# Moving output statistics, fusion and two projections within a hand-ordered schedule of attention and scans

## The chip, the cores and the metric

One core of a Trainium2 chip runs one program for the whole computation. The metric is the device time of one execution in microseconds (us), as the median of several runs. The engines are named as in the profile: PE (matmuls), DVE (vector), ACT (activations), POOL (GpSimd) and SP, whose queue issues the DMAs.

## The reference, cut to what matters

x is (8, 512, 48, 48), that is 8 samples of 512 channels by L = 2304 positions. Two layers follow each other, each with a group norm in front and a residual around it:

```python
# layer 0: linear causal attention, 8 heads of 64
Q = elu(Wq gn(x)) + 1;  K = elu(Wk gn(x)) + 1;  V = Wv gn(x)
S_t = S_{t-1} + k_t v_t^T;   o_t = (q_t S_t) / (q_t . cumsum(K)_t)
x = x + o
# layer 1: gn(x) in 4 blocks of 128 channels, one after the other
for i in range(4):
    x_i = spx[i] + prev                      # prev: the fused result of block i - 1
    xz = x_i @ Wi;  xp, z = split(xz)
    xs = silu(causal_conv4(xp));  dt, B, C = xs @ Wx
    delta = softplus(dt @ Wdt + b)
    h_t = exp(delta_t A) h_{t-1} + delta_t xs_t B_t      # 256 channels x 16 states
    y = (sum_n h_t C_t + xs D) * silu(z);  x_m = y @ Wo
    fg = max(x_i, x_m)
    prev = sigmoid(mean(x_i)) * x_i + sigmoid(mean(fg)) * fg
x = x + concat(prev of the four blocks)
```

The recurrence over positions is what DVE's scan instruction computes. The sigmoids' means are sums over all positions of a block, so a block's fusion starts only when all of its chunks are through; the next block of that sample starts from it. In the group norm in front of layer 1 each block needs the statistics of layer 0's output over all positions.

## The kernel before, in words

Positions are cut into NC = 6 chunks of LC = 384. The second layer's work comes in **jobs**: one chunk of one block of one sample, 8 x 4 x 6 = 192 jobs. A job has SLOTS = 8 **slots** (`slot(k)`), and a slot four scans of 128 x 384 (`scan`, L830). Each slot's body also makes, for slots ahead, the decays (`decay`, L819, an exponential on ACT into a PSUM bank), the products of B and delta x (`product` on DVE, L809, for most columns, `last_product` on POOL, L798, for the last 128), and behind the scans the weighing with C (`weigh`, L846, POOL), whose sum over states PE gathers into the one accumulator yp (`gather`, L853). yp is opened by the skip product (`skip`, L787, ACT) and emptied by the gate (`gated`, L865, DVE), twice a job. Two streams of samples take turns by job, so that one's fusion lies beside the other's scans.

Everything else is a *task*: a generator that yields where it may go on. A slot has two **halves**, and `beside(half)` is called in each, ahead of the first scan and behind the second; it lets each task that is due emit its next stage. `(t, gap), n` means: not before half t, at least gap halves after the last stage, with n free PSUM banks; a string of a digit is a gap alone. What is emitted this way stands in the engines' queues in that order, and no scheduler changes it. Half 0 to half 15 below are the halves of a job.

PSUM has six free banks, `take()`n and given back by tasks and decays. `ahead(DEPTH)` emits up to three decays ahead, as far as banks are there. Stores are kept in a list by `save` and issued on SP two halves later by `flush`.

The tasks that matter here:

- `chunk(m)` is layer 0 for one chunk of one block. `times[m]` is its first half, and falls into half 3 of a job in the steady part (a period of 16 halves); `at(j)` is half times[m] + j. It projects q, k and v (`project`, L286, three PSUM banks), forms q and k with an exponential and a relu on ACT (`feature`, L298 and L299) and a min and add on DVE (q L343, k L351), turns and sums (L362, L379), masks (L434) and adds the result to the input: `xr` at L450, its `bn_stats` at L452. After a block's last chunk `group_norm` aggregates them (L169), averages over 16 channels on PE (L171, L186), takes the power on POOL (L191) and leaves scale and shift (L195).
- `Stream.pass_on` fuses the finished block and prepares the next one's input xi, chunk by chunk: three DMA loads (xb, fu, xo; L569 to L574), scalings on ACT (L596, L597, L601), and additions on POOL (L604, L609, L612), or, for the first block of a sample, a normalization on ACT in place of L609 (L607). For a chunk c > 0 its times are given by `first`, the first half of the job that will need it.
- `Job.prepare` makes a later job's inputs: the conv (L635) and the gate's projection (L646) on PE, silu (L671 to L676, with a table load ahead of them and one behind) near half 14, the softplus (L706, again two table loads) near half 3, then the products of delta and xs on POOL (L747) and the loads of B, C, dr and dxr.
- `finale(job)` projects y with Wo (`project`, L871) and takes the maximum and its sum (`maximum`, L882). It is begun in half 4 of the next job, behind the last gate.

Of the kernel before, what the change touches and what calls it, by code (L numbers as in the profile page):

```python
# [49 lines left out]
def attention_then_mamba_kernel(  # L50
# [18 lines left out]
    B, _, L = x.shape  # L69
# [84 lines left out]
    def save(out, in_):  # L154
        stores.append((half_no[0], out, in_))

    def flush(every=True):
        while stores and (every or stores[0][0] <= half_no[0] - 2):
            _, o, i = stores.pop(0)
            nc.sync.dma_start(out=o, in_=i)  # L160
# [46 lines left out]
    norms, xns, x1s, done, ksums = {}, {}, {}, {}, {}  # L207
# [58 lines left out]
    def chunk(m):  # L266


        b, o, c = parts[m]
# [3 lines left out]
        cols, tile_rows = slice(c * LC, (c + 1) * LC), slice(o * P, (o + 1) * P)  # L273
# [3 lines left out]
        def at(j, gap=1):  # L277
            return times[m] + j, gap

        def new(tag, bufs=1, shape=(P, LC)):  # L280
            return apool.tile(list(shape), F32, tag=tag, name=f"{tag}_{n}", bufs=bufs)

        def project(j):
            ps = bank()[:, 0:LC]
            for kt in range(4):
                nc.tensor.matmul(  # L286
                    ps,
                    wq_sb[:, kt, j * 512 + o * P : j * 512 + (o + 1) * P],
                    xn[:, kt, :],
                    start=(kt == 0),  # L290
                    stop=(kt == 3),
                )
            return ps, bqkv_sb[:, j * 4 + o : j * 4 + o + 1]

        def feature(ps, bias):

            ex = new("ex", 2)
            nc.scalar.activation(ex, ps, AF.Exp, bias=bias)  # L298
            nc.scalar.activation(ps, ps, AF.Relu, bias=bias)  # L299
            return ex  # L300
# [31 lines left out]
        S, stats, ksum = passes[b, o]  # L332
# [5 lines left out]
        qp, qb = project(0)  # L338
        yield at(1), 0
        ex = feature(qp, qb)  # L340
        yield at(2), 0
        q = new("q", 2)
        nc.vector.scalar_tensor_tensor(q, ex, 1.0, qp, ALU.min, ALU.add)  # L343
        bank.free()
        yield at(2, 0), 1
        kp, kb = project(1)
        yield at(3), 0
        ex = feature(kp, kb)
        yield at(4), 0
# [73 lines left out]
        xr = new("xr")  # L423
# [25 lines left out]
        yield at(24), 0  # L449
        nc.vector.tensor_add(xr, xr, ops)  # L450
        bank.free()
        nc.vector.bn_stats(stats[:, 0, c, :], xr)  # L452
        save(x1s[b][tile_rows, cols], xr)
        if c + 1 == NC:
            norm = yield from group_norm(
                stats, 1, f"m{b}_{o}", 8, [(times[m] + j, 1) for j in (28, 29, 29, 30, 31)]
            )
            flush()
            done[b, o] = norm

    class Stream:
# [62 lines left out]
        def pass_on(self):  # L524


            xi = self.xi
            old = None
            if self.b is not None:
                old = self.b, self.s, self.n, self.fm  # L530
                wt = small.tile([P, 4], F32, tag="wt", name=f"wt_{self.n}")
                nc.vector.tensor_copy(wt[:, 2:3], self.sums)
                nc.vector.tensor_reduce(wt[:, 3:4], self.fsum, AX.X, ALU.add)
            last = old is not None and old[1] == 3 and not self.samples
            if not last:
                self.move_on()
                while (self.b, self.s) not in done:
                    yield "1w", 0
                norm = done[self.b, self.s]
            s = self.s  # L540
            if old is not None:
                yield "1", 0

                nc.scalar.activation(wt[:, 0:2], wt[:, 2:4], AF.Exp, scale=-1.0 / L)
                yield "1", 0
                nc.vector.tensor_scalar_add(wt[:, 0:2], wt[:, 0:2], 1.0)
                nc.vector.reciprocal(wt[:, 0:2], wt[:, 0:2])
            else:
                yield "1", 0
            if not last:  # L550
                if self.fresh:
                    self.sums = norm[:, 2, :]
                else:

                    sums = small.tile([P, 2], F32, tag="sums", name=f"sums_{self.n}", bufs=3)
                    nc.vector.tensor_scalar(
                        sums[:, 0:1], wt[:, 2:3], wt[:, 0:1], norm[:, 2, :], ALU.mult, ALU.add
                    )
                    nc.vector.tensor_scalar(
                        sums[:, 1:2], wt[:, 3:4], wt[:, 1:2], sums[:, 0:1], ALU.mult, ALU.add  # L560
                    )
                    self.sums = sums[:, 1:2]

            def loads(c):
                fu = xb = xa = None
                cols = slice(c * LC, (c + 1) * LC)
                if not last:
                    xb = mpool.tile([P, LC], F32, tag="xb", name=f"xb_{self.n}_{c}")
                    nc.sync.dma_start(out=xb, in_=x1s[self.b][s * P : (s + 1) * P, cols])  # L569
                if old is not None:  # L570
                    fu = mpool.tile([P, LC], F32, tag="fu", name=f"fu_{old[2]}_{c}")
                    nc.sync.dma_start(out=fu, in_=old[3][:, cols])
                    xa = mpool.tile([P, LC], F32, tag="xo", name=f"xo_{old[2]}_{c}")
                    nc.sync.dma_start(out=xa, in_=x1s[old[0]][old[1] * P : (old[1] + 1) * P, cols])  # L574
                return fu, xb, xa

            now = loads(0)
            for c in range(NC):

                if c and not last:  # L580
                    first = 2 * self.jobs[self.block * NC + c].start
                    yield (first - 36, 1), 0
                    now = loads(c)
                    yield (first - 30, 1), 0
                elif c:
                    yield "3", 0
                    now = loads(c)
                    yield "1", 0
                else:
                    yield "1", 0  # L590
                cols, icols = slice(c * LC, (c + 1) * LC), slice(3 + c * LC, 3 + (c + 1) * LC)
                fu, xb, xa = now
                if not last:
                    normed = dict(bias=norm[:, 1, :], scale=norm[:, 0, :])
                if old is not None:
                    nc.scalar.activation(fu, fu, AF.Copy, scale=wt[:, 1:2])  # L596
                    nc.scalar.activation(xi[:, icols], xi[:, icols], AF.Copy, scale=wt[:, 0:1])  # L597
                if old is None:
                    nc.scalar.activation(xi[:, icols], xb, AF.Identity, **normed)
                elif not last and not self.fresh:  # L600
                    nc.scalar.activation(xb, xb, AF.Identity, **normed)  # L601
                if old is not None:
                    yield "1", 0
                    nc.gpsimd.tensor_tensor(fu, fu, xi[:, icols], ALU.add)  # L604
                    yield "1", 0
                    if not last and self.fresh:
                        nc.scalar.activation(xi[:, icols], xb, AF.Identity, **normed)  # L607
                    elif not last:
                        nc.gpsimd.tensor_tensor(xi[:, icols], xb, fu, ALU.add)  # L609
                    self.ready = c + 1  # L610
                    yield "1", 0
                    nc.gpsimd.tensor_tensor(xa, xa, fu, ALU.add)  # L612
                    save(out[old[0], old[1] * P : (old[1] + 1) * P, cols], xa)
                self.ready = c + 1

    class Job:
# [250 lines left out]
        def project(self):  # L867
            self.bank = Banks()
            self.xm = self.bank()
            for h in range(2):  # L870
                nc.tensor.matmul(  # L871
                    self.xm[:, 0:LC],
                    self.w[2][:, h, :],
                    self.yz[:, h, :],
                    start=(h == 0),
                    stop=(h == 1),
                )
# [72 lines left out]
    parts, times = [], []  # L950
# [4 lines left out]
            parts.append((b, o, c))  # L955

    def finale(job):
        yield "0", 1
        job.project()
        yield "1", 0  # L960
        job.maximum()
        if job.c == NC - 1:
            yield from job.stream.pass_on()
# [4 lines left out]
    for b in counted:  # L968
        first = times[parts.index((b, 0, 0))]
# [59 lines left out]
    def at(k):  # L1029
        return jobs[k // SLOTS], k % SLOTS  # L1030
# [22 lines left out]
    def close(k):  # L1053

        job = at(k)[0]
        while waiting:
            waiting.pop(0)()
        job.gated(1)
        job.closed = True
        tasks.insert(0, Task(finale(job)))  # L1060
# [140 lines left out]
```

## Time and profile before

| | |
|---|---|
| median of 3 runs | 9154.76 us (9140.69 to 9157.51) |
| profiled execution, its own time | 9167.14 us |
| its span | 9165.3 us |
| granted TensorE clock, mean | 0.961 |
| DVE scans, L830 | 6144, 5471.0 us, 939 ns each |
| POOL weighing, L846 | 1536, 4880.6 us, 3177 ns each |
| ACT decays, L819 | 6144, 3432.3 us, 579 ns each |
| ACT table loads for L819, L671, L706 | 382, 192, 192, 1283 ns each |
| DVE statistics of the output, L452 | 192, 107.6 us, 560 ns each |
| HBM traffic | 178 GB/s over the span |

A group of instructions is given by its line, engine and operation. The table of waits says which engine waited, with the line of the instruction that waited and that of the one that released it, then the sum in us, the number of waits and the longest. In a timeline each row has a start and a duration in us, and idle time ahead of it in brackets.

### The profile page before, as it was taken

What the parts mean: (1) busy time and instruction counts of PE and PEld (TensorE: products, weight loads), DVE (VectorE), ACT (ScalarE), POOL (GpSimd) and SP (SyncE); (2) the same over time, 40 slices, a digit from 0 to 9 for tenths busy, and PEclk for the clock granted to TensorE, in tenths of its full rate; (3) what the DMA queues carried; (4) which work ended last, traced back from release to release, by engine and by line L of the source; (5) the groups of instructions that cost most, each with busy time, mean ns of one, the idle gap of its engine ahead of it and who ended that gap; (6) DMA issues with size and microseconds to landing.
All of it is one profiled execution on the core that took longest, in us unless ns stands there. A gap on an engine that the chain in (4) does not pass through costs nothing.

```text
span 9165.3 us, 120476 instructions
## 1 busy us (share of the span) xinstructions
PE 7631.5 (83%) x35714; PEld 3602.8 (39%) x35714; DVE 8342.1 (91%) x11640; ACT 6579.4 (72%) x12656; POOL 8066.8 (88%) x5635
## 2 busy tenths in 40 slices
PE   7888888888888888888888888888888888888865
PEld 4443444433344444443333444444333444444321
DVE  3899999999999999999999999999999999999997
ACT  2677777777777777777777777777777777777775
POOL 1788989899988899899998888998999898989998
PEclk9999999999999999999999999999999999999977
DMA  5566666666766666666666666666666666666654
GB/s 182 161 173 180 185 184 184 181 188 180 196 173 179 184 186 187 183 180 181 191 184 182 174 178 187 187 184 184 180 188 183 181 179 177 178 178 177 164 156 129
DMA packets 1002898, 1642.84 MB, mean 179 GB/s; under 512 B 138592, under 2 KB 797312, under 8 KB 1002240
## 3 DMA queue, kind: packets, MB, share of 16 engines
q1 hardware_dynamic: 1002240, 1635.13, 65.0%
q8 instruction: 283, 4.64, 0.2%
q14 instruction: 375, 3.07, 0.1%
HBM read 1309.06 MB, written 325.58 MB: 178 GB/s over the span
## 4 chain that ended last, share of the span: by engine, by line
DVE 31%; ACT 21%; PE 18%; POOL 10%; DMA 9%; issue 8%; SPq 3%; POOLq 0%; DVEq 0%; ACTq 0%
DVE u L830 20%; ACT bank L819 7%; PE bank L635 6%; POOL u L846 6%; DVE u L809 6%; PE bank L286 5%; ACT L819 4%; PE yp L853 3%; PE bank L646 3%; POOL u L798 2%; DMA C<-scr 2%; ACT L706 2%; ACT bank L299 1%; DMA B<-scr 1%; SPq L739 1%
## 5 line engine op out<-in xcount | busy, mean ns | idle before, releaser
L830 DVE TENSOR_TENSOR_SCAN u<-bank,u 128x385 f32<-128x385 f32 (+1 forms) x6144 | 5471.0, 939 | 378.3 <-ACT bank L819 331.9
L846 POOL TENSOR_TENSOR u<-u,C 128x1536 f32<-128x1536 f32 x1536 | 4880.6, 3177 | 216.4 <-DVE gm_m L175 83.2
L819 ACT ACTIVATE bank<-dr,av 128x385 f32<-128x385 f32 (+1 forms) x6144 | 3432.3, 579 | 1406.9 <-DVE u L830 1118.1
L853 PE MATMUL yp<-u,cst 128*64 128x384 f32 x12288 | 2429.2, 516 | 505.7 <-ACT yp L787 263.9
L798 POOL TENSOR_TENSOR u<-B,dxr 128x512 f32<-128x512 f32 x1536 | 1958.8, 1275 | 21.4 <-DMA dxr<-xscr 16.9
L809 DVE TENSOR_TENSOR u<-B,dxp 128x1024 f32<-128x1024 f32 x1536 | 1835.0, 1195 | 9.4 <-ACT dxp L782 9.4
L286 PE MATMUL bank<-xn,wq_sb 128*128 128x384 f32 x4608 | 1730.3, 520 | 97.1 <-DVE u L830 40.4
L853 PEld LDWEIGHTS yp<-u,cst 128*64 128x64 f32 x12288 | 781.0, 139 | 1713.3 <-issue 1051.6
L635 PE MATMUL bank<-xi,wk 128*128 128x384 f32 x3072 | 1122.1, 509 | 306.1 <-ACT kl L383 234.3
L286 PEld LDWEIGHTS bank<-xn,wq_sb 128*128 128x128 f32 x4608 | 870.0, 199 | 894.6 <-DVE u L830 153.6
L635 PEld LDWEIGHTS bank<-xi,wk 128*128 128x128 f32 x3072 | 563.0, 193 | 878.2 <-ACT kl L383 351.5
L844 POOL COPY state<-u 128x4 f32<-128x4 f32 x1280 | 241.7, 189 | 538.4 <-DVE u L830 522.7
L298 ACT ACTIVATE ex<-bank,bqkv_sb 128x384 f32<-128x384 f32 x384 | 219.6, 572 | 520.1 <-PE bank L286 491.6
L747 POOL TENSOR_TENSOR delta<-delta,xs 128x384 f32<-128x384 f32 x384 | 384.6, 1002 | 141.6 <-DMA dscr<-delta 124.6
L819 ACT ACT_TABLE_LOAD x382 | 490.1, 1283 | 6.7
L787 ACT ACTIVATE yp<-xs,pv 128x384 f32<-128x384 f32 x384 | 222.7, 580 | 373.2 <-DVE yz L865 373.2
L871 PE MATMUL bank<-yz,wo 128*128 128x384 f32 x768 | 307.0, 517 | 55.5 <-DVE yz L865 36.7
L695 PE MATMUL bank<-dbc,wd 9*128 9x384 f32 x768 | 302.2, 513 | 3.2 <-ACT dbc L687 3.2
L646 PE MATMUL bank<-xi,wi 128*128 128x384 f32 x768 | 289.2, 498 | 14.3 <-ACT xs L671 14.3
L416 PE MATMUL bank<-cst,rdb 128*128 128x128 f32 x576 | 103.2, 290 | 228.3 <-DVE u L830 226.1
L447 PE MATMUL bank<-sm,v 128*64 128x128 f32 x2304 | 260.9, 305 | 33.8 <-DVE u L830 30.6
L682 PE MATMUL bank<-xs,wx 128*40 128x384 f32 x768 | 281.3, 489 | 0.8 <-DVE sm L434 0.8
(109 smaller groups left out, 7632.7 us busy)
## 6 DMA issues: line engine op xcount, KB each, us to landing
B<-scr SPq DMA_DIRECT2D x1536, 192.0 KB
C<-scr SPq DMA_DIRECT2D x1536, 192.0 KB
xn<-xn SPq DMA_DIRECT2D x192, 768.0 KB
dr<-dscr SPq DMA_DIRECT2D x768, 192.0 KB
dxr<-xscr SPq DMA_DIRECT2D x768, 192.0 KB
dscr<-delta SPq DMA_DIRECT2D x192, 384.0 KB
xscr<-delta SPq DMA_DIRECT2D x192, 384.0 KB
xn<-in_x SPq DMA_DIRECT2D x48, 768.0 KB
```

The lines of the kernel that those rows point to most:

```text
L286: nc.tensor.matmul(ps, wq_sb[:, kt, j * 512 + o * P : j * 512 + (o + 1) * P], xn[:, kt, :], start=(kt == 0), stop=(kt == 3),)
L635: nc.tensor.matmul(xc, wk[:, k, h * P : (h + 1) * P], xi[:, c0 + k : c0 + k + LC], start=(k == 0), stop=(k == 3),)
L646: nc.tensor.matmul(zp, wi[:, 256 + h * P : 256 + (h + 1) * P], xi[:, c0 + 3 : c0 + 3 + LC], start=True, stop=True,)
L695: nc.tensor.matmul(vp, wd[32:41, h * P : (h + 1) * P], dbc[32:41, :], start=True, stop=True)
L747: nc.gpsimd.tensor_tensor(delta[:, h, :], delta[:, h, :], xs[:, h, :], ALU.mult)
L798: nc.gpsimd.tensor_tensor(u[:, :, :, 1 + LC - TAIL :], self.B[s % 4][:, :, cols].unsqueeze(2).to_broadcast(shape), self.dxr[s // 4][:, :, ...
L809: nc.vector.tensor_mul(u[:, :, :, 1 : 1 + LC - TAIL], self.B[s % 4][:, :, cols].unsqueeze(2).to_broadcast(shape), self.dxp.unsqueeze(1).to ...
L819: nc.scalar.activation(dA[:, cols], self.dr[h][:, g, cols], AF.Exp, scale=self.w[6][:, 2 * h + g, q + j : q + j + 1],)
L830: nc.vector.tensor_tensor_scan(u[:, j, g, cols], dA[:, cols], u[:, j, g, cols], 0.0, ALU.mult, ALU.add,)
L846: nc.gpsimd.tensor_tensor(h, h, self.C[s % 4].unsqueeze(2).to_broadcast([P, NG, 2, LC]), ALU.mult)
L853: nc.tensor.matmul(self.yp[g * 64 : g * 64 + 64, 0:LC], pair_sum, u[:, j, g, 1:], start=False, stop=(s % 4 == 3 and j == NG - 1), skip_gro ...
L871: nc.tensor.matmul(self.xm[:, 0:LC], self.w[2][:, h, :], self.yz[:, h, :], start=(h == 0), stop=(h == 1),)
```

## The change

It moves stages; it adds and removes no instruction.

- k's projection on PE is emitted in half 4, right behind q's `feature`, rather than in half 5 behind q's min and add; it takes its PSUM bank there.
- The statistics of the output (L452) go from half times[m] + 24, where `xr` is formed, to times[m] + 28, which is half 15. The save of xr stays. The group norm's stages follow, its last one a half later.
- For a chunk c > 0 the fusion's loads go from first - 36 to first - 33 and its work from first - 30 to first - 25. For chunk 0 one gap of a half is dropped.
- `finale` begins a half later, in half 5.

```diff
@@ chunk
         ex = feature(qp, qb)
+        yield at(1, 0), 1
+        kp, kb = project(1)
         yield at(2), 0
         q = new("q", 2)
         nc.vector.scalar_tensor_tensor(q, ex, 1.0, qp, ALU.min, ALU.add)
         bank.free()
-        yield at(2, 0), 1
-        kp, kb = project(1)
         yield at(3), 0
         ex = feature(kp, kb)
...
         nc.vector.tensor_add(xr, xr, ops)
         bank.free()
+        save(x1s[b][tile_rows, cols], xr)
+        yield at(28), 0
         nc.vector.bn_stats(stats[:, 0, c, :], xr)
-        save(x1s[b][tile_rows, cols], xr)
         if c + 1 == NC:
             norm = yield from group_norm(
-                stats, 1, f"m{b}_{o}", 8, [(times[m] + j, 1) for j in (28, 29, 29, 30, 31)]
+                stats, 1, f"m{b}_{o}", 8, [(times[m] + j, 1) for j in (28, 29, 29, 30, 32)]
             )
@@ Stream.pass_on
                     first = 2 * self.jobs[self.block * NC + c].start
-                    yield (first - 36, 1), 0
+                    yield (first - 33, 1), 0
                     now = loads(c)
-                    yield (first - 30, 1), 0
+                    yield (first - 25, 1), 0
...
                     nc.gpsimd.tensor_tensor(fu, fu, xi[:, icols], ALU.add)
-                    yield "1", 0
+                    yield "1" if c else "0", 0
@@
     def finale(job):
-        yield "0", 1
+        yield "2", 1
         job.project()
         yield "1", 0
         job.maximum()
```

## Prediction, on record before the changed kernel was run

> **What bounds the kernel now.** I read the page first, then DVE's waits, then one job in order of time. Busy time and waits of DVE:
>
> ```profile
> PE 7631.5 (83%) x35714; PEld 3602.8 (39%) x35714; DVE 8342.1 (91%) x11640; ACT 6579.4 (72%) x12656; POOL 8066.8 (88%) x5635
> ...
> DVE u L830 <- ACT bank L819: 331.9, 198, 4.4
> DVE k L351 <- ACT bank L299: 142.0, 135, 5.3
> DVE norm_m L195 <- POOL norm_m L191: 43.4, 31, 2.2
> DVE xr L450 <- PE bank L447: 40.2, 16, 8.8
> ...
> DVE u L830 <- POOL state L844: 25.0, 70, 0.4
> ```
>
> DVE carries the scans and is the fullest; POOL is close behind. DVE waits for POOL hardly anywhere, so DVE's own work plus the waits above sets the pace. Where these waits sit I got by lining up the middle 160 of 192 jobs (20 to 179) on the end of each job's eighth scan, called t = 0; times "at t" below are means of this. A job takes 46.5 us and has 16 halves of two scans each. DVE idles 3.04 us in it: 1.56 ahead of the last scan (half 15), 0.72 ahead of k's min/add (half 7), 0.24 ahead of a norm (half 3, only in jobs that end a block), 0.22 ahead of the ninth scan (half 4), 0.10 ahead of xr's addition (half 11). The largest, in one job (job 101, t = 0 at 4942.12), from ACT's and DVE's timelines (start, duration, engine, line, operation; idle time ahead of it in brackets):
>
> ```profile
> 4974.00 1.28 ACT L671 ACT_TABLE_LOAD   x1
> ...
> 4977.39 1.28 ACT L819 ACT_TABLE_LOAD   x1
> 4978.68 1.09 ACT L819 ACTIVATE bank<-dr,av 128x385 f32<-128x385 f32 x2
> ...
> 4976.32 0.95 DVE L830 TENSOR_TENSOR_SCAN u<-bank,u 128x385 f32<-128x385 f32 x1
> 4979.30 1.81 DVE L830 TENSOR_TENSOR_SCAN u<-bank,u 128x385 f32<-128x385 f32 x2 [2.03 <-ACT bank L819]
> ```
>
> The last decay stands behind two table loads and four silus: DVE is idle whatever it does. The k wait, in the same job, from the timeline and the clock table by windows:
>
> ```profile
> 4943.16 1.51 PE L871 MATMUL bank<-yz,wo 128*128 128x384 f32 x4
> 4946.66 2.75 PE L853 MATMUL yp<-u,cst 128*64 128x384 f32 x8 [1.98 <-ACT yp L787]
> 4949.34 3.26 PE L286 MATMUL bank<-xn,wq_sb 128*128 128x384 f32 x8
> ...
> 4953.69 0.55 DVE L351 SCALAR_TENSOR_TENSOR k<-ex,bank 128x384 f32<-128x384 f32 x1 [2.33 <-ACT bank L299]
> ...
> 4946.60:4949.40 2.80, 2.74 (x9) 0.92 (x9) 2.80 (x5) 2.55 (x6) 2.80 (x4) 0.53 0.25 93
> ```
>
> PE finishes the output's projection, idles 1.98 us until ACT's skip product has opened yp, and then runs the gather and k's projection behind it at a granted clock of 0.53. k comes late.
>
> **What the Trainium skill says.** "TensorE: Matmul & The Clock Gate", section "What's actually happening": the array falls to half clock after an idle window of about 3.4 us. The trace agrees in kind, not in size: 0.53 after 1.98 us here. Same page, section "Architectural detail": DVE and ACT are strictly first in, first out; the trace agrees, k's 2.33 us hold up the scans behind it. "ScalarE: Activation LUTs", section "What ACT_TABLE_LOAD costs": 1283 ns and a drain of about 1380; the page has 1283 ns and no drain is seen, the silu starts at 4975.30. "SBUF — State Buffer", section "SBUF: two separate sides": DVE instructions with two SBUF inputs and POOL's lock each other out. The ones moved here read one SBUF tensor, or PSUM and SBUF, so I price them alike in every half.
>
> **The change, part by part.** Nothing is added or removed; every queue keeps its instructions. The order of the two programs shows, in every steady job, these moves.
>
> *Statistics* (BATCH_NORM_STATS2, 0.56 us and 0.03 idle): from half 11 to half 15, behind the product and ahead of the last two scans. Half 11 loses 0.59 us, 113 us over 192 jobs. In half 15 it runs inside the wait. ACT's chain there is tied to the scan that frees a bank at the end of half 12: decays, copies, two loads, four silus, decay, 8.5 us (27.7 to 36.2 at t), against 7.0 us of DVE work. So it moves forward with DVE, and 0.59 fits in 1.56. Job by job 186 of 192 waits exceed 0.59; capping each at 0.59 gives **110 us**. The cover left is 1.0 us; without it, nothing is gained. x1's store now follows the addition alone, at the same place of SP's queue. The aggregation of a block's last chunk goes a half later, to half 0: 27 small groups of under 1 us, nothing.
>
> *Norm*: its power (POOL, 0.55 us) is issued in half 3 behind the next slot's product (L798, 1.28 us), and DVE needs it in half 4. DVE asked for it at -3.5 and it ended at -2.1. Now it ends 1.28 later, at -0.8, and DVE asks behind two scans, the product and the gate (1.85 + 1.20 + 0.55), at 0.1: no wait, **43 us**, at worst 0.
>
> *Fusion of chunks 1 to 5* (160 jobs). Its three ACT products (0.61 + 0.60 + 0.69 = 1.9 us) leave the place ahead of softplus and go between decays 16 and 17. Before, ACT ran without a gap from t = -5 to 4; that is what made the ninth scan wait 0.36 us in 97 of 160 jobs (shown as POOL state L844, 25.0, and issue, 11.7, though the decay ended 0.09 us before). **37 us.** At the new place scan 17 has 3.05 us in hand. On POOL, L604, L609, L612 (1.0 us each) leave slots 1 and 2 for slots 4 and 5. POOL then ends weigh(3) at about 16 (12.6 for the scans, 0.3, 3.2), adds fu by 17.2, L798 by 18.5, xi by 19.5; up to 22 in jobs with conversions of xn. The conv needs xi at 21, and may slip to 23.7 (2.85 + 1.06 us ahead of ACT's copies at 27.6). So the loads: SP issues xb, fu and xo three halves later, with eight halves instead of six before use. Cost: a fresh block's L607 waits on ACT for POOL's fu, some 36 jobs times 0.5 us, **-18 us**. SP's output store waits for L612 at t of about 25, ahead of x1's store and B's third load; B's use is four halves off, so nothing. For chunk 0, everything up to xi ends in the same half as before.
>
> *k's projection and the output's projection*: PE's order ahead of the first gather becomes rb, q, k, and xm stands behind it, ahead of the scores. q ends at 1.2 (median), k at 4.0, gather (1.51) at 5.5, xm (1.45) at 7.0. k's wait goes: +142 us. fg, its reader, stands in half 6 behind the product, and DVE is there at about 7.16. Job by job, with the warm durations, xm is late by 0.23 us on average (q runs cold in a quarter of the jobs): -44 us; two scans and k's min and add stand behind fg on DVE, and ACT's decays wait for the banks of those scans. If the gathers stay as slow as the 45 of 180 slow ones, it is late by 0.7, and nothing is left. But k fills the hole that cooled the array. **98 us**, bounds 0 and 142. PE's scores come 1.9 us sooner, so the masks are safe; fm's store is issued behind fg, and the next in SP's queue (xscr) waits longer, to 11, for POOL's delta.
>
> Sum: 110 + 43 + 37 - 18 + 98 = 270. DVE would then need 45.1 us a job; POOL is busy 42.0 (8066.8 / 192) and now waits 4.0 + 0.5, of which 2.7 around the last scan stay. That leaves it 1.8 us for 1.4 us, which in jobs with xn's conversions is too little: I take off 10%, to **244 us**. Against the profiled execution (9167.1, span 9165.3) that is 8923; its 12.4 us over the median of the runs shown (9154.8) go off as well: **8910**.
>
> **The rivals.**
> - *fg's wait takes the place of k's* (PE stays cold): 110 + 43 + 37 - 18 = 172, some 10% less, 155: **9000**. For it: fg has 1.2 us of cover where k had two scans and a product more. Against: 135 k waits, but only the 47 jobs with cold gathers have 2.0 us; the others 0.23.
> - *POOL becomes the bound*: of its 4.5 us it can give up only 0.5 a job: 96 us, **9060**. For it: 88% busy, and jobs 91 and 93 show no POOL wait at all. Against: its lag is made up in the next job (7.4 us of waits in job 92).
> - *xi too late* (slower): if ACT's scaled fu and xi, or POOL's backlog, bring xi at 26 rather than 19.5 to 22, conv(0), the turned k and v, silu and the last decay are late by 2.3 us in 160 jobs: 368 - 270 = 98 more, **9250**. It decides from xi at 25.4 on (270 / 160 = 1.7). Against: POOL's chain above.
> - *Nothing is moved*: the order of the instructions excludes it; that the moves cancel, **9155**, is left.
>
> **How the numbers follow.** Forecast 0.50 (own range 8850 to 8980); fg's wait 0.22; POOL 0.13; cancelling 0.05; xi 0.10. A measurement can tell 0.2%, 18 us, from no change. Faster is the first three, 0.85; same 0.05; slower 0.10. The range 8840 to 9110 takes in the first three and the bounds of 0 and 142 for k, and leaves out the last two and a little below.
>
> **What would show it.** Right: DVE's waits for L351 nearly gone and some 40 us ahead of L882; L195's and the ninth scan's gone; the last scan's wait near 1.0 us; the gathers near 1.5 us with the clock at 1.0. Wrong: L882 waiting for over 100 us, DVE waiting for POOL's L798, PE's L635 for xi, or the last scan's wait as large as before.

## The result, and the profile after

The changed kernel takes **9112.24 us** (median of 6 runs, 9105.45 to 9127.47) against 9149.0 us of the kernel before on the same chip (6 runs): ratio 0.9961, interval 0.9948 to 0.9974. It is faster, by 0.4% where I had forecast 2.7% (8910), and just outside the range that ended at 9110. The profiled execution's span is 9104.1 us at a mean clock of 0.959 (before 9165.3, 0.961).

Line numbers from 453 on are one higher than before (the scan L830 is now L831, the last decay L820, softplus L707, the gather L854, the output's projection L872, fg L883); q's last step went from L343 to L345 and the statistics from L452 to L454, while k's (L351), xr's product (L447) and xr (L450) keep theirs. The page's busy line of after, and DVE's waits (us in total, times, longest):

```profile
PE 7677.9 (84%) x35714; PEld 3678.4 (40%) x35714; DVE 8353.0 (92%) x11640; ACT 6588.8 (72%) x12656; POOL 8061.1 (89%) x5635
```

```profile
DVE u L831 <- ACT bank L820: 271.4, 192, 4.6
DVE q L345 <- ACT bank L299: 122.5, 62, 6.0
DVE fg L883 <- PE bank L872: 85.7, 86, 2.8
DVE stats_a L239 <- DMA xs<-in_x: 53.2, 31, 3.7
DVE xr L450 <- PE bank L447: 34.0, 16, 7.2
...
DVE u L831 <- POOL u L799: 14.3, 17, 1.8
DVE gm_m L188 <- PE bank L186: 11.6, 29, 1.6
```

k's wait (142.0) is 7.9 now, the norm's (43.4) 4.5, the ninth scan's (38.9 over all jobs) 0.8, and that of a job's last scan alone fell by 81 us, from 306 to 225. So of the waits that the forecast had named some 290 us are gone. But q's rose from 36.3 to 122.5, fg's from 1.4 to 85.7, the input statistics' (L239) from 25.5 to 53.2, scans 20 to 23 of a job (counted from 0) waited 30 more, and DVE is busy 11 us *longer* although it has the same instructions.

Where that happens shows when jobs are sorted by their number mod 6. In the middle 160 jobs a block ends every sixth job, so each class meets the same tasks. Mean length of a job in us, from the end of the last scan of the job before to that of its own:

| class | 0 | 1 | 2 | 3 | 4 | 5 |
|---|---|---|---|---|---|---|
| before | 46.72 | 45.70 | 48.65 | 45.66 | 46.13 | 46.27 |
| after | 46.76 | 45.98 | 51.44 | 43.91 | 45.47 | 44.06 |
| statistics alone | 45.35 | 45.24 | 48.19 | 44.57 | 45.51 | 44.66 |
| after, norm without its first gap (e1) | 46.83 | 46.32 | 48.32 | 43.91 | 45.48 | 44.07 |

Classes 3 to 5, ordinary jobs, gained up to 2.2 us. Class 2, where the norm, the last chunk's maximum and the pass to the next block fall, lost 2.79 us. One such job (job 68, t = 0 at 3379.37), from PE's and DVE's timelines of after, with PE's clock in the first window between (its length, the busy times of PE, PEld, DVE, ACT and POOL, then the granted clock, the DMA share and GB/s):

```profile
3371.67 1.55 PE L696 MATMUL bank<-dbc,wd 9*128 9x384 f32 x4
3376.87 0.59 PE L186 MATMUL bank<-gm_m,cst 128*128 128x1 f32 x2 [3.65 <-ACT delta L707]
3377.39 2.83 PE L854 MATMUL yp<-u,cst 128*64 128x384 f32 x8
3380.15 0.90 PE L416 MATMUL bank<-cst,rdb 128*128 128x128 f32 x3
3380.84 5.72 PE L286 MATMUL bank<-xn,wq_sb 128*128 128x384 f32 x16
```

```profile
3376.90:3379.90 3.00, 3.00 (x10) 1.24 (x10) 2.67 (x5) 2.97 (x6) 2.92 (x5) 0.50 1.09 304
```

```profile
3385.08 0.55 DVE L345 SCALAR_TENSOR_TENSOR q<-ex,bank 128x384 f32<-128x384 f32 x1 [1.72 <-ACT bank L299]
...
3389.53 0.56 DVE L883 SCALAR_TENSOR_TENSOR fg<-bank,xi 128x384 f32<-128x384 f32 x1 [1.07 <-PE bank L872]
```

The norm's second group mean (L186), a product of one column, waits 3.65 us for softplus. It does not read softplus's output; its PSUM bank is the one that softplus still has to empty, the first of L696's two. Followed through the kernels' `take` and `free`, 30 of the 32 second means of layer 1's norms get a bank that softplus read last, and before none. In the kernel before it stands a half earlier and runs without a wait, here in job 68 of before (t = 0 at 3404.38):

```profile
3396.97 0.38 PE L186 MATMUL bank<-gm_m,cst 128*128 128x1 f32 x2
3397.29 1.51 PE L853 MATMUL yp<-u,cst 128*64 128x384 f32 x8
```

In after it is at the head of PE's queue, so PE stands idle, and the gather behind it takes 2.83 us in place of 1.51, at a granted clock of 0.50. q's projection starts 1.5 us behind t = 0; in most other jobs it starts 1.6 us ahead of it. Once started, q's and k's projections take 5.72 us, hardly more than the usual 5.43: they are late because of the stall and the slow gather ahead of them. DVE then waits 1.72 us for q, and later 1.07 for fg.

The second loss of class 2 is in DVE's busy time: the 1 + exp of the sigmoids in the pass to the next block (L547, L546 before). From DVE's timeline, and POOL's at the same moment:

```profile
3396.13 1.57 DVE L547 TENSOR_SCALAR wt<-wt 128x2 f32<-128x2 f32 x1
```

```profile
3394.50 3.17 POOL L847 TENSOR_TENSOR u<-u,C 128x1536 f32<-128x1536 f32 x1
```

Two columns take 1.57 us, and end at 3397.70, when POOL's weighing (to 3397.67) is over. Over 32 blocks the row is 1488 ns each, against 334 before (10.7 to 47.6 us in all). 29 of the 32 steps come while a weighing runs, and each of these ends 22 to 29 ns behind that weighing; before, 24 of 32 do so too, but come shortly ahead of its end. The Trainium skill, "SBUF — State Buffer", section "Who interferes with whom", says that DVE in its two-port mode and POOL contend for one pair of ports and that the second to issue "fully blocks". That this step runs in that mode is not shown; if it does, its ends agree with the page to 0.03 us. The later finale moved it to an earlier point of a weighing: with the finale back (e4) it takes 424 ns.

### The profile page after: what moved, and what is told of

It reads as the page before. It is cut to its first block, busy times and chain, and to the rows that moved or that the text cites. A ratio compares the mean times of both kernels' runs of the same rounds, so it can differ in the third digit from the quotient of the medians.

```text
span 9104.1 us, 120479 instructions
## 1 busy us (share of the span) xinstructions
PE 7677.9 (84%) x35714; PEld 3678.4 (40%) x35714; DVE 8353.0 (92%) x11640; ACT 6588.8 (72%) x12656; POOL 8061.1 (89%) x5635
## 4 chain that ended last, share of the span: by engine, by line
DVE 35%; PE 15%; POOL 14%; DMA 12%; ACT 11%; issue 7%; SPq 6%; POOLq 0%; DVEq 0%; ACTq 0%
DVE u L831 22%; POOL u L847 9%; DVE u L810 6%; PE bank L286 4%; ACT bank L820 4%; PE yp L854 3%; PE bank L636 3%; SPq L740 3%; POOL u L799 2%; ACT L820 2%; DMA B<-scr 2%; DMA dscr<-delta 2%; DMA C<-scr 2%; ACT L707 2%; DMA wk<-in_wconv 1%
## 5 line engine op out<-in xcount | busy, mean ns | idle before, releaser
L831 DVE TENSOR_TENSOR_SCAN u<-bank,u 128x385 f32<-128x385 f32 (+1 forms) x6144 | 5466.4, 937 | 286.6 <-ACT bank L820 271.4
L820 ACT ACTIVATE bank<-dr,av 128x385 f32<-128x385 f32 (+1 forms) x6144 | 3442.9, 579 | 1451.1 <-DVE u L831 1110.6
L854 PE MATMUL yp<-u,cst 128*64 128x384 f32 x12288 | 2449.5, 521 | 338.0 <-POOL u L847 294.6
L286 PE MATMUL bank<-xn,wq_sb 128*128 128x384 f32 x4608 | 1632.6, 504 | 72.1 <-POOL xn L310 35.1
L854 PEld LDWEIGHTS yp<-u,cst 128*64 128x64 f32 x12288 | 772.8, 140 | 1556.8 <-issue 868.0
L447 PE MATMUL bank<-sm,v 128*64 128x128 f32 x2304 | 265.1, 309 | 77.8 <-DVE u L831 74.9
L429 PE MATMUL bank<-q,k 64*128 64x128 f32 x2304 | 267.3, 297 | 68.2 <-DVE fg L883 66.1
L696 PE MATMUL bank<-dbc,wd 9*128 9x384 f32 x768 | 309.6, 523 | 1.1 <-ACT dbc L688 1.1
L872 PE MATMUL bank<-yz,wo 128*128 128x384 f32 x768 | 305.2, 521 | 0.0
```

Source lines behind the costliest of these rows:

```text
L286: nc.tensor.matmul(ps, wq_sb[:, kt, j * 512 + o * P : j * 512 + (o + 1) * P], xn[:, kt, :], start=(kt == 0), stop=(kt == 3),)
L696: nc.tensor.matmul(vp, wd[32:41, h * P : (h + 1) * P], dbc[32:41, :], start=True, stop=True)
L820: nc.scalar.activation(dA[:, cols], self.dr[h][:, g, cols], AF.Exp, scale=self.w[6][:, 2 * h + g, q + j : q + j + 1],)
L831: nc.vector.tensor_tensor_scan(u[:, j, g, cols], dA[:, cols], u[:, j, g, cols], 0.0, ALU.mult, ALU.add,)
L854: nc.tensor.matmul(self.yp[g * 64 : g * 64 + 64, 0:LC], pair_sum, u[:, j, g, 1:], start=False, stop=(s % 4 == 3 and j == NG - 1), skip_gro ...
L872: nc.tensor.matmul(self.xm[:, 0:LC], self.w[2][:, h, :], self.yz[:, h, :], start=(h == 0), stop=(h == 1),)
```

## The experiments

Each kernel ran against the kernel before on the same chip, in several rounds. "Against before" is the difference of the two medians; the intervals of the ratios are 8 to 15 us to either side, so two kernels of this table that lie less than some 17 us apart are not told apart.

| kernel | us | against before | ratio, interval |
|---|---|---|---|
| after | 9112.2 | -37 | 0.9961, 0.9948 to 0.9974 |
| e1 norm without its first gap | 9026.9 | -134 | 0.9854, 0.9840 to 0.9867 |
| e2 fusion as before | 9207.4 | +46 | 1.0053, 1.0040 to 1.0065 |
| e3 1 + exp on ACT | 9099.7 | -62 | 0.9935, 0.9921 to 0.9948 |
| e4 finale as before | 9134.4 | -27 | 0.9976, 0.9967 to 0.9984 |
| e5 fusion of chunks 1 to 5 as before | 9074.1 | -79 | 0.9912, 0.9899 to 0.9926 |
| e6 weights later | 9108.4 | -45 | 0.9947, 0.9934 to 0.9959 |
| e8 maximum later | 9078.4 | -75 | 0.9915, 0.9902 to 0.9929 |
| e9 before + statistics | 8999.0 | -154 | 0.9833, 0.9820 to 0.9847 |
| e10 e9 + fusion | 9011.5 | -142 | 0.9842, 0.9828 to 0.9855 |
| e11 e9 + k and finale | 9167.6 | +14 | 1.0012, 1.0003 to 1.0020 |
| e12 e9 + norm's last step later | 8968.7 | -185 | 0.9795, 0.9781 to 0.9808 |
| e13 after, mended | 8913.7 | -240 | 0.9739, 0.9726 to 0.9752 |
| e14 e11 + chunk 0's gap of 0 | 9031.6 | -120 | 0.9864, 0.9848 to 0.9881 |
| e15 e14, k as before | 9431.1 | +279 | 1.0302, 1.0287 to 1.0317 |
| e17 e9 + the change's norm chain | 9068.9 | -83 | 0.9906, 0.9891 to 0.9920 |

### Parts of after undone

**e1: the norm without its first gap.** Each step stands at least a gap of one half behind the one before it. Without the gap ahead of the first step the first four come a half earlier; the last step falls into half 33 in both kernels.

```diff
-stats, 1, f"m{b}_{o}", 8, [(times[m] + j, 1) for j in (28, 29, 29, 30, 32)]
+stats, 1, f"m{b}_{o}", 8, [(times[m] + j, int(j > 28)) for j in (28, 29, 29, 30, 33)]
```

> The changed kernel, with the block's aggregation in the same half as its last statistics, so that the norm's two small matmuls (L171, L186) stand on PE where they stood before and L186 takes a bank that no softplus holds; the last stage stays where the change puts it. Theory A (PE's stall of 3.7 us behind L186, waiting for softplus's bank, in the 32 jobs that end a block, is what ate the gain there): DVE's waits for q fall by about 1.4 us and those ahead of fg by 0.8 us in these jobs, some 80 us in all: 9030. Rival B (POOL is the bound since the fusion moved): the stall goes, but DVE waits elsewhere: 9095 to 9115. The wait for the norm's power stays gone under both.

Measured: 97 us better than after. Class 2 falls from 51.44 to 48.32 us (3.12 x 32 = 100), its q wait from 1.47 to 0.01 us a job; L186 has no wait for softplus any more, and none of these products gets a bank that softplus read last. The bank is the cause. q's and k's projections take longer here in class 2 than in after (median 7.12 against 5.50 us), and still q is not waited for: it was late by the stall. The wait of fg (88.2, 80 times) stays, but for 0.27 us a job in class 2: it is not due to the norm.

**e2: the whole fusion back**, chunk 0's gap included.

```diff
-yield (first - 33, 1), 0
+yield (first - 36, 1), 0
...
-yield (first - 25, 1), 0
+yield (first - 30, 1), 0
...
-yield "1" if c else "0", 0
+yield "1", 0
```

> The changed kernel with the fusion of chunks 1 to 5 where it was before (36 and 30 halves ahead, and chunk 0's gap back). Theory A (the fusion's POOL work now meets the scaling of the next weights, and POOL's weighing and PE's gathers fall behind in one job of six): waits for q and fg fall by 66 us in those jobs and those for the statistics' load by 24, while the ninth scan's wait comes back with 37: 9060 to 9080. Rival B (the fusion's move is a plain gain of ACT time): 37 us and more are lost, 9150.

Measured: 83 us worse than after. Classes 0, 1 and 2 got 38, 33 and 52 us better in all, and class 3 went from 43.91 to 50.58 us a job, 213 us worse: neither theory had that. PE's waits have a new row, L416 for softplus (104.4 us, 29 times), which e11 explains. Two edits were undone at once here; e5, e11 and e14 take them apart.

**e3: 1 + exp of the pass on ACT**, away from DVE.

```diff
 nc.scalar.activation(wt[:, 0:2], wt[:, 2:4], AF.Exp, scale=-1.0 / L)
+nc.scalar.activation(wt[:, 0:2], wt[:, 0:2], AF.Identity, bias=1.0)
 yield "1", 0
-nc.vector.tensor_scalar_add(wt[:, 0:2], wt[:, 0:2], 1.0)
```

> The changed kernel with the 1 + exp of the fusion's weights made on ACT (one more activation of 128x2 behind the exponential), and DVE's tensor_scalar of 128x2 left out. Theory A (that instruction, 0.33 us before and 1.49 us now, stands behind POOL's weighing, whose end it takes to finish, so a lock between the two engines costs 1.2 us in 32 jobs): DVE's busy time falls by 48 us, time by 35 to 45: 9070. Rival B (DVE has slack there, and the time is waited for elsewhere): 9105 to 9115.

Measured: DVE's busy time falls by 46 us, the scans' wait for decays rises from 271.4 to 299.9, and 25 us remain, with some 17 of uncertainty. About half of DVE's 46 us was on the path; class 2 ends in the wait for ACT's last decay (1.68 us a job in after, 2.65 here), which takes the rest. The run shows what the step costs, not by which mechanism it is held.

**e4: the finale back** to the half before (`yield "0", 1`). k's projection then finds no bank ahead of the first gather and stands behind it, as before. But it stands ahead of q's last step in the source, so its delay goes on to what follows: q's last step comes in half 6 rather than 5, k's exponential in 7 rather than 6, k's last step and v's projection in 8 rather than 7. e4 is thus more than the two moves undone.

> The changed kernel with the output's projection a half sooner, as before. The projection takes the bank that k's projection would need, so k's projection stands behind the first gather again, as before: both parts of the projections' move are undone. Theory A (k's wait of 142 us was only changed for one ahead of fg, 86, and q, 123, and for the lock, 37): k's wait comes back with about 130 us, fg's and a third of q's and the lock go: 9100 to 9130. Rival B (k's move pays in full, and what ate the gain lies elsewhere): 9210.

Measured: 10 us worse than after, which the intervals do not separate. q's wait falls to 33.6 us, and k's stays at 8.6, where theory A had 130. Two things favour k here: with the fusion off ACT's queue yp opens sooner (PE waits 74.1 us for it, 263.9 before) and slow first gathers (over 1.7 us) fall from 53 of 192 before to 5; and k's last step has a half more of cover. e10, where k's steps stand as before, tells them apart. In their place xr waits 144.8 us for its product, 134 times, and fg 118.0 us, 58 times, more than in after.

**e5: the fusion of chunks 1 to 5 back**, chunk 0's gap kept (the first two pairs of lines of e2).

> After with the fusion of chunks 1 to 5 put back to where before has it (36 and 30 halves ahead in place of 33 and 25); chunk 0 keeps its gap of 0, so its job's first loads stay where after has them. Theory A (GpSimd's slots 5 and 6 of a job's last half and the class of jobs 1 carry two adds and the scaling of the weights; and Scalar's queue ends the last scan's wait): jobs of classes 0 and 1 give back 20 to 45 us each, class 2 some 20 us, the wait of the statistics' first reduction falls from 53 to about 25 us; the wait at the ninth scan comes back (0.8 to about 30 us). Class 3, which the joint edit of the earlier run raised by 213 us, stays at about 44 us a job. Span 9000 to 9050 us, ratio 0.984 to 0.989. Theory B (the class 3 loss of the earlier run comes from the fusion of chunks 1 to 5 itself, and not from chunk 0's gap): class 3 rises to some 50 us a job again, and the time is 9180 to 9210 us.

Measured: 42 us better than after, a little less than theory A had. q's wait in class 1 falls by 1.09 us a job, the statistics' load wait in class 0 by 0.73, and class 3 stays at 44.40; class 2 gives nothing back (51.42). So the fusion's new place costs more than the ninth scan's wait it removes. What PE waits for, in after:

```profile
PE yp L854 <- POOL u L847: 294.6, 282, 5.0
...
PE bank L636 <- POOL xi L610: 125.7, 80, 3.8
```

and in e5:

```profile
PE yp L854 <- POOL u L847: 251.9, 274, 6.0
...
PE bank L636 <- POOL xi L610: 30.8, 24, 3.9
```

In after PE stands 125.7 us for xi ahead of the conv (54.8 in the kernel before), and 43 us longer for POOL's weighing than in e5: POOL's backlog reaches PE.

**e6: the weights' scaling four halves later** (first `yield "3", 0` of `weights` to `"7"`).

> After with the scaling of the next block's weights begun four halves later, so that GpSimd's four products of a block lie in other slots than the fusion of a chunk. Theory A (the scaling, 4 x about 1 us in the slots that the moved fusion took, holds back the weighing, and with it the gathers and q's projection of class 1): q's and fg's waits in class 1 fall by about 2 us a job, 32 jobs: 65 us, so 9050 us, ratio 0.993 to after. Theory B (class 1 waits for the fusion's own two adds): within 15 us of after, 9095 to 9130 us.

Measured: 8 us better than after, nothing that can be told. Theory A is not borne out at this distance. But the trace shows two thirds of the scaling still in the first four slots of class 1, and the last part beside that class's own fusion, so the run moves the load rather than removes it.

**e8: the maximum of chunks 0 to 4 a half later.**

```diff
 job.project()
-yield "1", 0
+yield "2" if job.c + 1 < NC else "1", 0
 job.maximum()
```

> After with the maximum of chunks 0 to 4 of a block a half later (two halves behind the output's projection in place of one); the last chunk's stays. Theory A (fg's wait of 86 us, 86 times, is the projection standing a half later behind the gathers with no half between it and its reader): the wait falls below 15 us and the time by 60 to 80 us: 9030 to 9050 us. Theory B (the half by which it is late only moves to what stands behind, the next slot's scan, or to the store of fm and the load of fu behind it): fg's wait goes, and the waits of the last scan or of the fusion grow by as much; 9095 to 9130 us.

Measured: 38 us better than after; fg's wait falls from 85.7 to 33.8 us, and those left are the last chunk's in class 2, which keeps its place. That is theory A's mechanism, with three fifths of the wait and half of the time that it gave.

### Parts of the change alone, on the kernel before

**e9: the statistics alone**, with the norm's chain as it was.

```diff
-nc.vector.bn_stats(stats[:, 0, c, :], xr)
 save(x1s[b][tile_rows, cols], xr)
+yield at(28), 0
+nc.vector.bn_stats(stats[:, 0, c, :], xr)
...
-[(times[m] + j, 1) for j in (28, 29, 29, 30, 31)]
+[(times[m] + j, int(j > 28)) for j in (28, 29, 29, 30, 31)]
```

> Before with one part of the change alone: each chunk's statistics over x1 in the silu slot (at(28)), the chain of the norm in its old places, its first step without a half's gap. Theory A (the statistics leave the wait for xr's product, and stand where Vector waits for Scalar anyway): the last scan's wait falls by 80 to 110 us and nothing else moves by 15 us: 9040 to 9075 us. Theory B (what the silu slot gives is taken back in q's and fg's waits, since Scalar and the tensor engine set the pace there): 9130 to 9165 us, with q's wait up from 36 us by 50 us or more.

Measured: 154 us better than the kernel before, more than either theory had, and four times what the whole change gives. DVE's waits in this kernel:

```profile
DVE u L831 <- ACT bank L820: 250.7, 199, 4.4
DVE k L351 <- ACT bank L299: 75.7, 136, 4.8
DVE norm_m L195 <- POOL norm_m L191: 43.1, 31, 2.2
DVE q L343 <- ACT bank L299: 42.3, 17, 6.0
DVE xr L450 <- PE bank L447: 29.3, 14, 7.2
```

The scans' wait for decays, mostly the last scan's, falls by 81 us, as theory A said, and k's by 66, which neither theory said. PE still waits about as long for yp to open (263.9 us before, 257.8 now), but fewer of the first gathers behind that wait run slow: 18 of 192 in place of 53. Of those with 1.75 to 2.25 us of idle time ahead of them, 7 of 97 take over 1.7 us, and before 43 of 106.

**e17: the same with the norm's chain as in the change** (every step with a gap of one half, the last not before 32, which with the gaps is half 33).

> Before with the statistics in the silu slot and the norm's chain as the change has it (each step with a half's gap, the last at 32); nothing else. Theory A (the half's gap ahead of the first step lets the second group mean take the bank that softplus holds, whatever the other three parts do): against the statistics with the old chain (8999 us) class 2 gets some 2.5 us a job slower, net of the 43 us that the norm's later last step saves: 9035 to 9080 us, with the wait of that product for softplus near 3.5 us. Theory B (the bank falls so only with the other parts): 8955 to 8990 us.

Measured: 71 us worse than e9, as theory A said. PE's waits show the bank without any other part of the change:

```profile
PE bank L186 <- ACT delta L707: 108.8, 30, 3.7
```

In e9 L186 has no such row; in after the row is 109.2 us, 30 times.

**e12: e9 with the norm's last step at 33** (with its gaps it fell into 32 in e9), nothing else.

> Before with the statistics in the silu slot and the norm's last step two halves later (33 in place of 31), the rest of its chain in its old places, and nothing else. Theory A (Vector's wait for GpSimd's root, 43 us in 31 places of class 2, is on the path that ends the job, and the norm has no reader for which the two halves are too late): 43 us less than with the statistics alone: 8950 to 8965 us. Theory B (class 2 waits for the last scan's Scalar drain, 2.0 us a job, as long anyway): within 12 us of 8999 us.

Measured: 31 us better than e9, where theory A had 43. The norm's wait went (43.1 us), and part came back: the pass's 1 + exp met a weighing here too (0.30 to 1.10 us a job in class 2). Between e12 and e17, the half's gap ahead of the aggregation costs 102 us (e1 gave 97).

**e10: e9 with the fusion moved.**

> Before with the statistics in the silu slot (norm chain in its old places) and the fusion at 33 and 25 halves with chunk 0's gap of 0; k's projection and the output's projection where before has them. The statistics alone took 9153 to 8999 us. Theory A (the fusion is worth what it frees, the waits of k, 76 us, and of the ninth scan, some 37 us, less what scans 20 to 23 and the statistics' loads take back, some 55 us): 8930 to 8960 us, k's wait below 10 us. Theory B (with the fusion GpSimd's and Scalar's order pushes the attention chunk's tensor work behind late gathers, the wait of xr for its product that the run with the finale put back showed at 145 us): 9030 to 9060 us, xr's wait above 100 us and k's still below 10 us.

Measured: 12 us worse than e9, which the intervals do not separate, and neither theory's number. PE waits 68.6 us for yp to open (e9 257.8), k's wait falls from 75.7 to 26.9 us without k being moved, and the ninth scan's goes, while q's wait rises from 42.3 to 97.0 (1.33 us a job in class 1), the statistics' loads from 25.2 to 50.3; xr stays at 34.9, so theory B's wait does not come from the fusion alone; e4, where it was seen, differs from e10 by the half by which q's and k's later steps and v's projection are late, and by the norm's chain. Which of these brings xr's wait is not shown.

**e11: e9 with k and the finale moved.** **e14: the same with chunk 0's gap of 0.** **e15: e14 with k where it was.**

> Before with the statistics in the silu slot (old norm chain), k's projection ahead of q's last step and the output's projection a half later than the gathers' end; the fusion where before has it. Theory A (the projection moved behind the gathers makes a block's last chunk pass on a half later, so xi and the next job's preparation and q are late in the job behind it, as the run with the fusion put back showed): 9100 to 9130 us, q's wait above 120 us, class 3 of jobs above 48 us each. Theory B (the two moves are worth what their waits promise: k's wait of 76 us falls to below 15 us, nothing behind it): 8930 to 8950 us.

> The statistics with k's and the output's projections moved (9168 us) and chunk 0's gap of 0 in the pass from block to block added; the fusion's halves as before. Theory A (class 3 lost 6.1 us a job there because chunk 0's xi, and with it the next preparation and the bank that softplus holds, came a half later; the gap of 0 gives that half back): class 3 returns to 44 us, 32 x 6.1 = 195 us less: 8965 to 8985 us. Theory B (the later preparation has another cause): 9140 to 9175 us.

> The same without k's move: k's projection stays behind q's last step, which puts its second half behind a slot's first gather again, in every middle job. Theory A (k's move is what empties k's wait): k's wait 60 to 90 us, and 50 to 75 us slower than with the move, 9025 to 9050 us. Theory B (k's wait is emptied by the output's projection that no longer stands ahead of k in the tensor engine's queue, and the move itself gives nothing): k's wait below 15 us and within 15 us of the run with the move.

e11 measured: 168 us worse than e9, with class 3 at 50.86 us a job (e9: 44.57). From PE's timeline of e11 in such a job (job 75, t = 0 at 3719.39), and its sum over all jobs:

```profile
3720.16 0.55 PE L416 MATMUL bank<-cst,rdb 128*128 128x128 f32 x3 [3.75 <-ACT delta L707]
3720.55 7.12 PE L286 MATMUL bank<-xn,wq_sb 128*128 128x384 f32 x16
```

```profile
PE bank L416 <- ACT delta L707: 99.5, 29, 3.8
```

The same mishap with another victim: chunk 0's xi comes a half later, the preparation that waits for it follows, and now rb (L416) takes the bank that softplus holds, in 29 jobs by the kernel's `take` and `free`. It is the row that e2 had. e14 has no such row, class 3 is back at 44.39 us as theory A said, and the time 134 us better, not 195. What is left, 34 us against e9, lies in class 2 (1.71 us a job, the others hardly differ): 1.19 us of it is the longer 1 + exp, and 0.53 the later scans' waits for decays. k's wait is gone in e14, and fg's is 55.5 us where e9 has next to none.

e15 measured: 400 us worse than e14, far beyond both theories; k waits 244.4 us, in all classes, and fg 230.2, in all but class 2. From PE's timeline of e15:

```profile
3829.88 1.51 PE L854 MATMUL yp<-u,cst 128*64 128x384 f32 x8 [3.33 <-ACT yp L788]
3831.32 1.56 PE L872 MATMUL bank<-yz,wo 128*128 128x384 f32 x4
3832.72 2.74 PE L286 MATMUL bank<-xn,wq_sb 128*128 128x384 f32 x8
```

PE idles 3.33 us and then has the gather, the output's projection and k's in a row, with k last. k's move and the finale's belong together: the output's move without k's takes the time to 279 us above the kernel before, though the statistics are moved too, and both together still cost 34 us on the statistics. k's move alone was not run.

### Mended

**e13: after with e1's, e3's, e5's and e8's edits together.**

> After with four repairs at once: the norm's first steps without a half's gap (worth 86 us alone), 1 + exp of the pass from block to block on Scalar (13 to 28 us), the fusion of chunks 1 to 5 back at 36 and 30 halves (38 us) and the maximum of chunks 0 to 4 a half later (34 us). Theory A (the four pay for separate waits: norm's bank, the lock of the shared port, the queue of Scalar and GpSimd, the projection behind the gathers): they add up to 170 to 185 us, so 8925 to 8945 us. Theory B (what one mends, another's wait covers: all end in the same waits of q and the last scan): half of it, 9000 to 9030 us, no better than the statistics alone (8999 us).

Measured: 240 us better than the kernel before and 203 better than after. The four repairs measured one by one against after give 97 + 25 + 42 + 38 = 202 us, so within the intervals they pay for separate waits, as theory A said. DVE's waits of e13:

```profile
DVE u L831 <- ACT bank L820: 265.2, 206, 4.4
DVE q L345 <- ACT bank L299: 40.5, 18, 6.0
DVE xr L450 <- PE bank L447: 36.6, 15, 8.8
DVE stats_a L239 <- DMA xs<-in_x: 25.9, 15, 3.7
DVE u L831 <- POOL state L845: 25.8, 70, 0.7
DVE fg L883 <- PE bank L872: 25.2, 24, 2.8
```

It is the fastest kernel here. It keeps, of the change, the statistics, k's and the output's projections and chunk 0's gap; the fusion of the other chunks is where it was. From e12 it differs by k's and the output's projections, chunk 0's gap and the edits of e3 and e8, and it is 55 us faster. Part of that can be e3's edit, as the 1 + exp takes 33.2 us of DVE in e12; with the two repairs the projections' move seems to pay, but no run sets it apart.

## Why the prediction was wrong, step by step

The waits to be removed were read rightly and most went. What failed is what the sum took to be free: chiefly the norm's steps, moved by a half at a price of nothing. The forecast missed after by 202 us, as much as the four repairs of e13 give back. That e13 lands on the forecast (8914 against 8910) is partly luck: it leaves the fusion's move out, the statistics gave more than their price, and the norm gave less.

- **Statistics, priced at 110 us.** Alone they give 154. The wait for decays, 81 us less, is below the 110; k's wait adds 66. k's 142 us was booked in full to k's move, so 66 us of it were not that move's to give once the statistics had moved. That k's wait would shrink with the statistics was in no term.
- **Norm, priced at 43.** The last step's delay is worth 31 (e12), some of the rest going to a longer 1 + exp. The sentence that failed is "The aggregation of a block's last chunk goes a half later, to half 0: 27 small groups of under 1 us, nothing": the step costs nothing by its duration, and some 100 us (e1 97, e17 against e12 102) by the place in PE's queue and in the rotation of banks that it gives L186. I counted the instructions that move, and not which bank each would then get. This is the largest term of the miss.
- **Fusion of chunks 1 to 5, priced at 37 - 18.** The ninth scan's wait went as said (38.9 to 0.8). The fresh block's wait was not 0.5 us in 36 jobs, 18 in all: ACT stood 126.9 us in 36 places (L608 for L605; L607 22.3 us before), and DVE 28 us ahead of scan 21 in nine jobs, up to 4.6 us each. On the statistics alone the move gives nothing that can be told (e10), and in after it costs 42 us (e5). The failed step is the 10% taken off for POOL: a mean over jobs hid classes 0 and 1, where xi and the weighing come late and PE waits for both. They have the weights' scaling besides; e6, which moved it, gained nothing that can be told, so its part is not shown. "So nothing", for SP's output store, failed with it: SP stood 961.5 us behind L613 in place of 423.4, and the statistics' loads (L239), which were not in the sum, were waited for 28 us longer at DVE. In class 0 of the middle jobs DVE waited for ten of them; ahead of each SP had stood 6.1 to 6.4 us for L613, until some 27 to 29 us behind t = 0, and the load went out 0.3 to 2.0 us after that. In e5 SP still waits 917.9 us for L613, but at another half, and the loads' wait is back at 26.2.
- **k's and the output's projections, priced at 98.** k's wait fell by 134 us. (The clock of 0.53 that the forecast gives for the gather and k's projection is the gather's: over k's projection, 4949.40 to 4952.60, it is 0.88, and the 3.26 us stand against a usual 2.85.) fg's rose by 84 where I had 44. And "The ones moved here read one SBUF tensor, or PSUM and SBUF, so I price them alike in every half" held for the statistics (560 ns before, 550 after) and failed on a small step behind the finale, the 1 + exp of the pass, which reads one SBUF tensor: it costs 37 us more of DVE, and its duration depends on where in a weighing it comes. (No run here tests two SBUF inputs, the case that the forecast cites.) On top of the statistics the pair, with chunk 0's gap of 0, costs 34 us (e14 against e9).
- **Chunk 0**, "everything up to xi ends in the same half as before": right, and worth far more than I knew. Without the gap of 0 the same pair costs 134 us more (e11 against e14).
- **The rivals.** None came alone. fg's wait did take part of the place of k's (85.7 of 142 us), POOL did bind in two classes, and xi was late in some jobs (125.7 us at the conv), but not in all 160, for which the slower rival asked. A wait for a bank was in none of them.

Still open is why the first gathers run slow less often once the statistics are moved (53 to 18), with PE's idle time ahead of them almost unchanged (254.6 and 248.5 us). Open too is how much of k's 66 us comes from this.

## What to carry to other kernels

In a schedule written out by hand, a step that moves by a half also moves in the rotation of shared buffers: for each moved step look up whose buffer it takes and when that is empty, however short the step is. Sum gains by kind of job, not over the mean job, and where two parts of a change work on the same wait, book it once. When several small moves come together, try each alone first: here one of the four alone gave four times what all of them did.

## What the runs showed of the hardware

- A one-column product, 0.38 us long in the kernel before, held PE for 3.65 us, as softplus had still to empty its bank; afterwards the granted clock was 0.50 and the gather took 2.83 us in place of 1.51. The profile puts the wait down to softplus, whose result the product never reads.
- The DVE operation on 128 x 2 elements took 334 ns on average before and 1488 ns after. Where it came during a weighing of POOL (24 and 29 of 32 times), it ended 22 to 31 ns behind it, so its length is what was left of the weighing.
- With an idle time of 1.75 to 2.25 us ahead of it, a first gather sometimes took 1.5 us and sometimes up to 2.8: moving the statistics alone took those over 1.7 us from 43 of 106 to 7 of 97.
